# First mixer of an eight-layer kernel: reordering around the FIR filters, their sums on GpSimd, and bands with four channels innermost

## The chip, the cores and the metric

The kernel runs on one core of a Trainium2 chip, as one program. The metric is the device time of one execution in microseconds. The engines are PE (TensorE, its weight loads listed as PEld), DVE (VectorE), ACT (ScalarE), POOL (GpSimd) and SP (SyncE, which here only issues DMAs). Each engine works through its own queue in order; a DMA issued from SP's or ACT's queue runs on the core's 16 DMA engines.

## The reference

Four pairs of a token mixer and a feed-forward layer act on `x`, each as `x = x + layernorm(f(layernorm(x)))`. The change is in the first mixer only. `x` has 8 batches (the leading shape is 8 x 512 tokens x 256 channels here). Cut to what matters:

```python
q, k, v = (silu_short_conv(x @ W.T, conv) for each of the three)    # 4 taps, causal
delta = delta_rule_chunkwise(q, k, v, sigmoid(x @ Wb.T))            # 4 heads of 64; needs, per chunk of 32,
                                                                   # the inverse of a 32 x 32 triangle
fs, fm, fl = fir(v, 3 taps), fir(v, 15 taps), fir(v, 63 taps)       # causal, one filter per channel
g = softmax_with_floor(gate(x))                                    # 5 weights per head and token
o = g[0] * fs + g[1] * fm + g[2] * fl + g[3] * delta + g[4] * v
return rmsnorm(o) @ Wo.T
```

## The kernel before

The kernel is written in a tile framework. The order of the program text gives instructions their priority; a scheduler at compile time then orders each engine's queue, by what it takes to be ready, and places the semaphores. So an instruction can stand in its queue earlier than its text.

The mixer `l0_attn` has three stages, and `K.XA`, the buffer of the 8 batches of X (64 KB of each partition), is lent out in all of them.

**The front** (`front(b)`, 8 batches): normalisation and transposes, projections on PE, short convolutions on DVE (line 456), ACT's activations, shifted copies of v in `Vw` (line 488), and k k^T of every chunk in `S`, written to DRAM (`s_d`, lines 505 and 509). `front` is a generator and yields 11 times a batch. Per batch the rows of gates and strengths go to DRAM as `rows_d` (line 469).

Each half of the batches has one **inverse**: `inverse(0)` uses `K.XA[:, 0:4]`, `inverse(1)` `K.XA[:, 4:8]`. Its generator loads 2 MB of `s_d` (line 331) and the strengths `gb` from `g_d`, multiplies (line 343), makes 30 steps of a forward substitution on DVE (lines 351 and 354), multiplies again (line 357), and ends with a tail: an `affine_select` and a copy on POOL (lines 360 and 363), one 2 MB write to `t_d` on SP (line 364), and four times a transposing copy `tt` on ACT with a 512 KB write to `tt_d` on ACT's queue (lines 367 and 368; two buffers). `strengths(g)` makes `g_d` for a half: two loads from `rows_d`, a Tanh on ACT, four operations of DVE, four writes on SP (lines 377 to 388). `inverse(0)` starts after batch 3 and takes one step at each yield of batches 4 to 7, tail included. `strengths(1)` follows batch 7.

**The filters** (`filters(g)`, 32 groups of 8 channels). Channels are filtered as matmuls: lhsT is a strided slice of `Vw` (64 columns), rhs a band matrix of taps. The bands live in DRAM as `fd` and are read in windows by `load_toep` into three rotating tiles `toep` (two of them lie in `K.XA[:, 4:8]`). A tile has 4 filters (short, middle, long, identity) x 64 shifts x 8 channels, channels innermost, so one channel's 256 columns lie 8 floats apart:

```python
rhs=toep[g % NB_T][:, :, :, c],
```

Two matmuls of 64 columns each (r = 0, 1) go to the two halves of a PSUM bank. Per half group DVE multiplies the bank with the gates `gt` (line 632, tile `pr`, two buffers), then DVE adds the four products in two steps, `s1` (line 638) and `s2` (line 640), and ACT's queue writes `s2` to `f_d` (line 642). PSUM has 6 banks for this, so three groups. The gates of a head (`gates(h)`, lines 567 to 585) come from `rw_all`, which two DMAs load from `rows_d` (line 553). `scaled_v` (line 612) writes `v_d` every fourth group. After group 0 `load_tt` loads the transposed inverses of batches 0 and 1 (line 401).

After the last group the text has, in this order: `inverse(1)` started (its 2 MB read first), the four X loads of the first half, the buffers of the back half, and the loads of batches 0 and 1.

**The back half** (`back(b)`): the two halves of each inverse are joined (tile `W`, line 741, and `TT`, line 755), then the sequential part per batch; `inverse(1)` takes one step in two turns of the loop and is finished by force before batch 4's loads.

Of the kernel before, what the change touches and what calls it, by code (L numbers as in the profile page):

```python
# [9 lines left out]
F32 = mybir.dt.float32  # L10
# [264 lines left out]
def l0_attn(K):  # L275
# [6 lines left out]
    with ExitStack() as es:  # L282
# [45 lines left out]
        def inverse(g):  # L328
# [17 lines left out]
            for j in range(1, 31):  # L346
# [11 lines left out]
                both, both, blocks(gb, 0, (32, 2), (0, 32), (1, 32)), ALU.mult)  # L358
            yield
            nc.gpsimd.affine_select(  # L360
# [45 lines left out]
        with ExitStack() as e1:  # L406
            pv = pool(e1, "v", 1)
            Vw = pv.tile([P, NB, J, D], F32, name="Vw")
            with ExitStack() as ef:
# [11 lines left out]
                for f, (col, taps) in enumerate(((A_FS, 3), (A_FM, 15), (A_FL, 63))):  # L421
                    at = 1536 * f + 8 * (P - taps)
                    nc.sync.dma_start(
                        out=window(fd, 1536 * f, (4608, G), (1, 8 * (P - taps))),
                        in_=zero[:, 0:8 * (P - taps)])
                    nc.sync.dma_start(
                        out=window(fd, 1536 * f + 1024, (4608, G), (1, 512)), in_=zero[:, 0:512])
                    nc.sync.dma_start(
                        out=window(fd, at, (8, taps), (4608, G), (1, 8)),
                        in_=taps_T[col - A_FS:col - A_FS + taps].rearrange("u (g c) -> u g c", c=8))  # L430

# [80 lines left out]

                inv = iter(())
                for b in range(NB):
                    for _ in front(b):
                        next(inv, None)
                    if b % HALF == HALF - 1:
                        strengths(b // HALF, p1)
                    if b == HALF - 1:
                        inv = inverse(0)  # L520
                        next(inv)

            with ExitStack() as ef:
# [6 lines left out]
                for i in range(NB_T):  # L530
                    if i < 2:
                        t = K.XA[:, HALF + 2 * i:HALF + 2 * i + 2].rearrange(
                            "p b n d -> p (b n d)").rearrange("p (f t c) -> p f t c", f=4, c=8)
                    else:
                        t = p1.tile([P, 4, 64, 8], F32, name=f"toep{i}")
                    nc.gpsimd.memset(t, 0.0)
                    nc.vector.tensor_copy(
                        t[:, 3],
                        K.ident[:, 64:128, None][:, ::-1, :].to_broadcast([P, 64, 8]))
                    toep.append(t)  # L540

                def load_toep(g):
                    t = toep[g % NB_T]
                    nc.sync.dma_start(
                        out=t[:, 2].rearrange("p t c -> p (t c)"),
                        in_=window(fd, (3 * g + 2) * 1536, (8, P), (1, 512)))
                    nc.sync.dma_start(
                        out=t[48:128, 0:2].rearrange("p f t c -> p f (t c)"),
                        in_=window(fd, 3 * g * 1536 + 384, (8, 80), (1536, 2), (1, 512)))

# [67 lines left out]
                def filters(g):  # L618
# [3 lines left out]
                    for half in range(2):  # L622
                        ps = pmm.tile([P, 2, 4, 64], F32, tag="fir", name=f"pf{g}_{half}")
                        for m in range(2):
                            for r in range(2):
                                c = 4 * r + 2 * half + m
                                nc.tensor.matmul(
                                    ps[64 * r:64 * r + 64, m],
                                    lhsT=Vw[:, :, :, 8 * g + c].rearrange("p b j -> p (b j)"),
                                    rhs=toep[g % NB_T][:, :, :, c],  # L630
                                    start=True, stop=True)
                        nc.vector.tensor_tensor(
                            pr[:, 2 * half:2 * half + 2], ps[:, :, :, ::-1],
                            gt[:, h, None].to_broadcast([P, 2, 4, 64]), ALU.mult)
                    if g + NB_T < G:
                        load_toep(g + NB_T)
                    s1 = p1.tile([P, 4, 2, 64], F32, tag="s1", name=f"s1_{g}")
                    nc.vector.tensor_tensor(s1, pr[:, :, 0:2, :], pr[:, :, 2:4, :], ALU.add)
                    s2 = p2.tile([P, 4, 64], F32, tag="s2", name=f"s2_{g}")
                    nc.vector.tensor_tensor(s2, s1[:, :, 0, :], s1[:, :, 1, :], ALU.add)  # L640
                    for r in range(2):
# [4 lines left out]
                gates(0)  # L646
                given = False
                for g in range(G):
# [7 lines left out]
                    if g % 4 == 3:  # L656
                        scaled_v(g // 4)
                    if next(inv, 0) == 0 and not given:
                        given = True
                        for b in range(2):  # L660
                            load_tt(b)
        assert given
        inv = inverse(1)
        next(inv)
        K.load_x(K.i["x"], range(HALF))

# [206 lines left out]
        K.log_exp = True  # L873
        ahead = {b: loads(b) for b in range(2)}
        live, done, begun, steps = [back(0, *ahead[0])], 0, 1, 0
        while live:
# [1754 lines left out]
```

## Time and profile before

| | |
|---|---|
| median of 3 runs | 4565.85 us (4554.68 to 4568.97) |
| profiled execution | 4579.0 us, its span 4577.3 us |
| busy in the span | PE 3989.2 (87%), DVE 2710.9 (59%), POOL 2043.3 (45%), ACT 1982.9 (43%) |
| mean granted TensorE clock | 0.925 |
| the first mixer | from the start to about 710 us of the span |
| filters | first matmul at 248.8 us, last DVE product at 387.5 us |
| back half | first matmul at 402.7 us |

Times in the profile are microseconds from the span's start unless marked ns. A row of a group gives line, engine, operation, out<-in, shapes and count, then busy time and the mean ns of one, then the idle time of the engine before them and what ended it. In the timeline a row has its start, its length, the engine and in brackets the idle time before it and its releaser; SPq and ACTq are DMA issues. One fp32 matmul stands as two records.

### The profile page before, as it was taken

The page shows a single profiled execution, that of the slowest core. Times are in us where ns is not written, and L with a number is a line of the kernel's source. Part 1 is how long each engine was busy: PE and PEld are TensorE (multiplying, and loading weights), DVE is VectorE, ACT ScalarE, POOL GpSimd, SP SyncE. Part 2 cuts the span into 40 slices and gives each one's busy share as a digit, 9 for nine tenths or more (in the row PEclk, how much of TensorE's full clock was granted, in tenths as well). Part 3 has the DMA queues.
Part 4 walks back from the last instruction along what each step waited for, and adds up shares of the span by engine and source line. Part 5 has one row for each costly group of instructions (what it writes and reads, how often), then busy time and mean ns, then how long its engine had stood idle before and what let it go on. Part 6 is the DMA issues. An engine that isn't in the chain of part 4 may idle for free. (4 is left out here: it accounts for less than half of the span.)

```text
span 4577.3 us, 63200 instructions
## 1 busy us (share of the span) xinstructions
PE 3989.2 (87%) x21672; PEld 2642.3 (58%) x21672; DVE 2710.9 (59%) x7215; ACT 1982.9 (43%) x4082; POOL 2043.3 (45%) x2013
## 2 busy tenths in 40 slices
PE   8887898999998599789999978898988866899997
PEld 3435675555555399644454544565655544678884
DVE  7677656456647611255566534888888899721115
ACT  5511433444344233334444444767676655311112
POOL 0000322444344234345555423889888879223321
PEclk9897998999999799889999989999999986899999
DMA  4467621000000199500000002344333434236653
GB/s 117 142 180 193 174 50 45 18 10 6 7 5 20 52 249 251 148 5 10 6 6 6 1 23 67 122 125 127 124 123 121 125 106 138 93 121 230 228 182 113
DMA packets 389361, 442.89 MB, mean 97 GB/s; under 512 B 147469, under 2 KB 271487, under 8 KB 388527
## 3 DMA queue, kind: packets, MB, share of 16 engines
q1 hardware_dynamic: 361087, 390.18, 28.4%
q0 software_dynamic: 16272, 31.87, 2.6%
q10 hardware_dynamic: 11680, 16.80, 1.1%
q8 instruction: 172, 2.82, 0.3%
q14 instruction: 150, 1.23, 0.1%
HBM read 372.49 MB, written 66.26 MB: 96 GB/s over the span
## 5 line engine op out<-in xcount | busy, mean ns | idle before, releaser
L2046 POOL TENSOR_TENSOR h<-h,C 128x1024 f32<-128x1024 f32 x256 | 613.5, 2409 | 137.6 <-DVE h L2042 95.0
L2042 DVE TENSOR_TENSOR_SCAN h<-dA,dB 128x512 f32<-128x512 f32 x480 | 568.1, 1208 | 91.0 <-ACT dA L2030 77.3
L1000 POOL TENSOR_SCALAR p<-p,rs 128x128 f32<-128x128 f32 (+3 forms) x256 | 275.9, 1085 | 416.5 <-DVE rs L999 260.5
L2030 ACT ACTIVATE dA<-dl,A 128x512 f32<-128x512 f32 x480 | 330.5, 690 | 174.4 <-DVE h L2042 173.6
L1566 DVE CUSTOM_DVE_ANT_0 junk<-S,mask 128x256 f32<-128x256 f32 (+3 forms) x512 | 249.5, 487 | 195.1 <-PE S L1560 156.8
L2059 PE MATMUL y<-C,h 128*128 128x128 f32 x2048 | 295.3, 295 | 73.0 <-POOL h L2046 72.8
L2059 PEld LDWEIGHTS y<-C,h 128*128 128x128 f32 x2048 | 260.2, 153 | 158.5 <-POOL h L2046 102.9
L1594 ACT ACTIVATE PT<-T 128x128 f32<-128x128 f32 (+3 forms) x512 | 198.1, 435 | 278.9 <-PE T L1589 267.9
L1560 PE MATMUL S<-KZ,QT 64*128 64x512 f32 (+3 forms) x1024 | 260.1, 491 | 23.8 <-DVE mx L1566 23.6
L2258 PE MATMUL gb<-xbT,w_b 128*128 128x256 f32 (+1 forms) x1472 | 255.3, 332 | 1.0 <-ACT ts L2462 0.6
L2258 PEld LDWEIGHTS gb<-xbT,w_b 128*128 128x128 f32 x1472 | 230.2, 191 | 23.1 <-ACT ts L2462 0.8
L2264 DVE TENSOR_TENSOR hTb<-sb,gb 128x512 f32<-128x512 f32 x71 | 48.8, 687 | 325.4 <-PE gb L2258 314.1
L2025 POOL TENSOR_TENSOR dB<-du,B 128x1024 f32<-128x1024 f32 x96 | 233.8, 2436 | 0.1
L1844 PE MATMUL pf<-fT,w_l_ffn 128*128 128x512 f32 x384 | 206.6, 676 | 28.5 <-ACT fT L1838 11.3
L1589 PE MATMUL T<-QT,KZ 64*128 64x384 f32 (+3 forms) x1024 | 217.1, 465 | 2.9 <-ACT PT L1594 2.5
L2025 DVE TENSOR_TENSOR dB<-du,pb 128x1024 f32<-128x1024 f32 x160 | 191.2, 1195 | 23.4 <-ACT pb L2023 21.3
L182 POOL TENSOR_TENSOR X<-X,yn 128x256 f32<-128x256 f32 (+1 forms) x56 | 79.7, 1441 | 263.0 <-ACT yn L177 233.1
L1334 ACT ACTIVATE hT<-h,w_l_ffn 128x128 f32<-128x128 f32 x384 | 109.5, 368 | 198.0 <-PE h L1329 198.0
L1329 PE MATMUL h<-xgT,w 128*128 128x128 f32 x1536 | 185.1, 279 | 0.0
L1560 PEld LDWEIGHTS S<-KZ,QT 64*128 64x128 f32 x1024 | 116.7, 193 | 114.0 <-issue 58.3
L1597 POOL TENSOR_SCALAR_AFFINE_SELECT PT<-PT 128x512 f32<-128x512 f32 x128 | 81.3, 635 | 219.1 <-ACT PT L1594 206.2
L998 ACT ACTIVATE p<-p,nm 128x128 f32<-128x128 f32 (+3 forms) x256 | 143.5, 561 | 80.7 <-DVE nm L994 72.7
(587 smaller groups left out, 9147.0 us busy)
## 6 DMA issues: line engine op xcount, KB each, us to landing
w_b<-l3f_w SPq DMA_DIRECT2D x138, 512.0 KB
C<-xdd SPq DMA_DIRECT2D x256, 256.0 KB
B<-xdd SPq DMA_DIRECT2D x256, 256.0 KB
w<-l1f_w SPq DMA_DIRECT2D x48, 1024.0 KB
w<-l1f_w SPq DMA_DIRECT2D x48, 256.0 KB
X<-x SPq DMA_DIRECT2D x16, 512.0 KB
c<-ys SPq DMA_DIRECT2D x16, 512.0 KB
X<-l0fd SPq DMA_DIRECT2D x22, 320.0 KB
```

Source lines behind the costliest of these rows:

```text
L1000: nc.gpsimd.tensor_scalar(p[:, 0:n], p[:, 0:n], rs, None, ALU.mult)
L1560: nc.tensor.matmul(ps[:, 0:n], lhsT=QT[half, qt * P:n], rhs=KZ[half, j % 2, 0:n], start=True, stop=True)
L1566: nc.vector.tensor_tensor_reduce(out=junk[:, 0:n], in0=ps[:, 0:n], in1=mask[:, L - n:L], scale=1.0, scalar=-3.0e38, op0=ALU.add, op1=ALU.m ...
L1589: nc.tensor.matmul(ps[:, 0:n], lhsT=KZ[half, j % 2, kt * P:(kt + 1) * P], rhs=QT[half, kt * P:L], start=True, stop=True)
L1594: nc.scalar.activation(PT[:, j, :], ps[:, 0:n], AF.Exp)
L1844: nc.tensor.matmul(ps, lhsT=gu[:, k, j * 768 + c * P:j * 768 + (c + 1) * P], rhs=R[b]["fT"][:, k, :], start=(k == 0), stop=(k == 1))
L2025: on.tensor_tensor(dBs[k], R[b]["du", h], B[:, None, :].to_broadcast([P, 2, L]), ALU.mult)
L2030: nc.scalar.activation(dA, R[b]["dl", h][:, c, :], AF.Exp, scale=A[:, 2 * h + c, n:n + 1])
L2042: nc.vector.tensor_tensor_scan(hs[k][:, c, :], dA, dBs[k][:, c, :], 0.0, ALU.mult, ALU.add)
L2046: nc.gpsimd.tensor_tensor(hs[k], hs[k], row_C.pop(k)[:, None, :].to_broadcast([P, 2, L]), ALU.mult)
L2059: nc.tensor.matmul(R[b]["y", h][q // 2][:, q % 2, c * P:(c + 1) * P], lhsT=t[:, c, q * P:(q + 1) * P], rhs=K.ident, is_transpose=True, sta ...
L2258: nc.tensor.matmul(ps[:, q, :], lhsT=ww[:, k, (c + q) * P:(c + q + 1) * P], rhs=xT[:, k, :], start=(k == 0), stop=(k == 1))
```

## The change

Five things are changed in `l0_attn`. (1) `inverse` yields True ahead of its tail; the front stops stepping `inverse(0)` there, and the rest, with `load_tt` for batches 0 and 1, is run after group 1 of the filters. (2) `strengths(1)` is called after group 21 in place of after batch 7. (3) The X loads of the first half and the start of `inverse(1)` stand behind the loads of batches 0 and 1. (4) `s1` and `s2` are added on GpSimd. (5) The bands have their 8 channels split into two blocks (one for each r) of 64 shifts x 4 channels, so that a channel's columns lie 4 floats apart; `fd` is written with 16-byte pieces and read with 1 KB pieces.

```diff
@@ inverse
             nc.vector.tensor_tensor(
                 both, both, blocks(gb, 0, (32, 2), (0, 32), (1, 32)), ALU.mult)
-            yield
+            yield True
             nc.gpsimd.affine_select(
...
@@ the writes of fd
-                    at = 1536 * f + 8 * (P - taps)
+                    n = 4 * (P - taps)
                     nc.sync.dma_start(
-                        out=window(fd, 1536 * f, (4608, G), (1, 8 * (P - taps))),
-                        in_=zero[:, 0:8 * (P - taps)])
+                        out=window(fd, 1536 * f, (4608, G), (768, 2), (1, n)),
+                        in_=zero[:, 0:2 * n].rearrange("g (q n) -> g q n", q=2))
                     nc.sync.dma_start(
-                        out=window(fd, 1536 * f + 1024, (4608, G), (1, 512)), in_=zero[:, 0:512])
-                    nc.sync.dma_start(
-                        out=window(fd, at, (8, taps), (4608, G), (1, 8)),
-                        in_=taps_T[col - A_FS:col - A_FS + taps].rearrange("u (g c) -> u g c", c=8))
+                        out=window(fd, 1536 * f + 512, (4608, G), (768, 2), (1, 256)),
+                        in_=zero[:, 0:512].rearrange("g (q n) -> g q n", q=2))
+                    for q in range(2):
+                        nc.sync.dma_start(
+                            out=window(fd, 1536 * f + 768 * q + n, (4, taps), (4608, G), (1, 4)),
+                            in_=taps_T[col - A_FS:col - A_FS + taps].rearrange(
+                                "u (g q c) -> u g q c", q=2, c=4)[:, :, q])
...
@@ the loop over the front
                 inv = iter(())
+                inverted = True
                 for b in range(NB):
                     for _ in front(b):
-                        next(inv, None)
-                    if b % HALF == HALF - 1:
-                        strengths(b // HALF, p1)
+                        inverted = inverted or next(inv)
                     if b == HALF - 1:
+                        strengths(0, p1)
                         inv = inverse(0)
-                        next(inv)
+                        inverted = next(inv)
+                assert inverted
...
@@ bands
-                        t = p1.tile([P, 4, 64, 8], F32, name=f"toep{i}")
+                        t = p1.tile([P, 4, 2, 64, 4], F32, name=f"toep{i}")
...
                     nc.sync.dma_start(
-                        out=t[:, 2].rearrange("p t c -> p (t c)"),
-                        in_=window(fd, (3 * g + 2) * 1536, (8, P), (1, 512)))
+                        out=t[:, 2].rearrange("p q t c -> p q (t c)"),
+                        in_=window(fd, (3 * g + 2) * 1536, (4, P), (768, 2), (1, 256)))
                     nc.sync.dma_start(
-                        out=t[48:128, 0:2].rearrange("p f t c -> p f (t c)"),
-                        in_=window(fd, 3 * g * 1536 + 384, (8, 80), (1536, 2), (1, 512)))
+                        out=t[48:128, 0:2].rearrange("p f q t c -> p (f q) (t c)"),
+                        in_=window(fd, 3 * g * 1536 + 192, (4, 80), (768, 4), (1, 256)))
...
@@ filters
-                                    rhs=toep[g % NB_T][:, :, :, c],
+                                    rhs=toep[g % NB_T][:, :, r, :, 2 * half + m],
...
-                    nc.vector.tensor_tensor(s1, pr[:, :, 0:2, :], pr[:, :, 2:4, :], ALU.add)
+                    nc.gpsimd.tensor_tensor(s1, pr[:, :, 0:2, :], pr[:, :, 2:4, :], ALU.add)
...
-                    nc.vector.tensor_tensor(s2, s1[:, :, 0, :], s1[:, :, 1, :], ALU.add)
+                    nc.gpsimd.tensor_tensor(s2, s1[:, :, 0, :], s1[:, :, 1, :], ALU.add)
...
@@ the loop over the groups
-                    if next(inv, 0) == 0 and not given:
-                        given = True
+                    if g == 1:
+                        for _ in inv:
+                            pass
                         for b in range(2):
                             load_tt(b)
-        assert given
-        inv = inverse(1)
-        next(inv)
-        K.load_x(K.i["x"], range(HALF))
+                    if g == 21:
+                        strengths(1, p1)
...
@@ ahead of the back half
         ahead = {b: loads(b) for b in range(2)}
+        K.load_x(K.i["x"], range(HALF))
+        inv = inverse(1)
+        next(inv)
```

More of the change, by code (lines that the diff above doesn't have):

```diff
@@ L532, in l0_attn @@
                         t = K.XA[:, HALF + 2 * i:HALF + 2 * i + 2].rearrange(
-                            "p b n d -> p (b n d)").rearrange("p (f t c) -> p f t c", f=4, c=8)
+                            "p b n d -> p (b n d)").rearrange(
+                                "p (f q t c) -> p f q t c", f=4, q=2, c=4)
                     else:
-                        t = p1.tile([P, 4, 64, 8], F32, name=f"toep{i}")
+                        t = p1.tile([P, 4, 2, 64, 4], F32, name=f"toep{i}")
                     nc.gpsimd.memset(t, 0.0)
@@ L538, in l0_attn @@
                         t[:, 3],
-                        K.ident[:, 64:128, None][:, ::-1, :].to_broadcast([P, 64, 8]))
+                        K.ident[:, None, 64:128, None][:, :, ::-1, :].to_broadcast([P, 2, 64, 4]))
                     toep.append(t)
@@ L646, in l0_attn @@
                 gates(0)
-                given = False
                 for g in range(G):
```

## The prediction

> **What bounds the kernel now.** The change touches only the first mixer, so I read stretches of it, then the waits inside. The first two rows below are two batches of the front (batch 1, and batch 7); the others are the start of the filters, their steady part, and the gap before the back half. Columns: stretch and length, busy us of PE, PEld, DVE, ACT, POOL (with counts), PE clock, DMA share, GB/s.
>
> ```profile
> 38.56:64.83 26.27, 24.55 (x96) 11.73 (x96) 18.57 (x46) 16.16 (x28) 0.21 (x1) 0.94 0.30 74
> 202.38:241.60 39.22, 29.83 (x96) 14.65 (x96) 15.26 (x23) 23.38 (x32) 3.85 (x3) 0.78 0.62 196
> 256.00:279.00 23.00, 5.04 (x22) 2.08 (x20) 18.89 (x41) 2.11 (x3) 1.80 (x1) 0.66 0.93 263
> 279.00:388.00 109.00, 107.92 (x464) 46.74 (x460) 83.88 (x164) 0.94 (x2) 0.00 (x0) 0.98 0.64 193
> 388.00:403.00 15.00, 0.30 (x12) 0.34 (x14) 8.46 (x18) 1.28 (x1) 4.27 (x11) 0.55 0.81 238
> ```
>
> PE sets the front (24.6 of 26.3 us) and the filters (107.9 of 109). Three places break that: batch 7, 13 us longer than batch 1; the start of the filters; and the 15 us before the back half.
>
> Batch 7 first, by ACT's timeline:
>
> ```profile
> 206.12 3.77 ACT L367 COPY tt<-X 128x1024 f32<-128x1024 f32 x2 [0.60 <-POOL X L363]
> 213.73 1.91 ACT L367 COPY tt<-X 128x1024 f32<-128x1024 f32 x1 [2.81 <-DMA l0tt<-tt]
> 216.04 1.95 ACT L367 COPY tt<-X 128x1024 f32<-128x1024 f32 x1
> ```
>
> The four transposing copies that end `inverse(0)` sit in ACT's queue between the copies that empty PE's banks, and the third waits for a write of the first to land; DVE then waits 22.7 us in one piece for ACT (L454).
>
> PE's timeline at the start of the filters, and SP's:
>
> ```profile
> 248.84 7.71 PE L627 MATMUL pf<-X,Vw 128*64 128x256 f32 x32 [1.05 <-ACT S L502]
> 266.37 3.98 PE L627 MATMUL pf<-toep,Vw 128*64 128x256 f32 x16 [9.81 <-DVE rw_all L567]
> 278.50 7.68 PE L627 MATMUL pf<-X,Vw 128*64 128x256 f32 x32 [8.15 <-DVE pr L632]
> 251.81 3.95 SPq L388 DMA_DIRECT2D l0g<-bts  x4
> 257.21 1.16 SPq L553 DMA_DIRECT2D rw_all<-l0rows  x2
> ```
>
> PE fills its banks, then idles 9.8 + 8.2 = 18 us for the gates, whose input `rw_all` is issued only behind the four writes of `strengths(1)`.
>
> In the steady part, groups by line (busy, mean ns | idle before):
>
> ```profile
> L627 PE MATMUL pf<-X,Vw 128*64 128x256 f32 x320 | 76.4, 645 | 8.6 <-DVE pr L632 8.6
> L632 DVE TENSOR_TENSOR pr<-pf,gt 128x512 f32<-128x512 f32 x63 | 42.8, 685 | 16.5 <-PE pf L627 16.5
> L638 DVE TENSOR_TENSOR s<-pr 128x512 f32<-128x512 f32 x31 | 21.1, 681 | 0.0
> L640 DVE TENSOR_TENSOR s<-s 128x256 f32<-128x256 f32 x30 | 12.4, 412 | 4.1 <-DMA l0f<-s 4.1
> ```
>
> PE never waits for DVE for long there, and DVE's pr waits for PE. The pace is in the timeline of PE's weight loads:
>
> ```profile
> 301.35 0.20 PEld L627 LDWEIGHTS pf<-X,Vw 128*64 128x64 f32 x2 [0.26 <-issue]
> 301.82 0.20 PEld L627 LDWEIGHTS pf<-X,Vw 128*64 128x64 f32 x2 [0.26 <-issue]
> ```
>
> A pair of half-width matmul records starts every 0.465 us. A group has 8 matmuls of two records each, so 8 pairs: 8 x 0.465 = 3.72 us. Elsewhere pairs and fours of column halves run side by side at the speed of one: L1611's records of 256 contiguous columns come in fours 0.22 us apart, L193's singly 0.216. So these bands, read 32 bytes apart, cost 2.15 times a contiguous read.
>
> **The change part by part.** The profiled execution took 4579.0 us (span 4577.3, 1.7 around it), 13 above the median 4565.85 of the runs; I work out differences in the former and take them off the latter. A measurement can tell about 0.3%, 13.7 us, from nothing.
>
> *Tail of `inverse(0)`, moved behind group 1.* It issues POOL 4.07 + 0.37 us, a 2 MB write on SP, four ACT copies (7.7 us) and four 512 KB writes on ACT's queue; behind it `load_tt` puts four loads on SP. Batch 7 loses its excess over batches 1 to 3 (26.3, 25.3, 26.5; mean 26.0): 39.2 - 26.0 = 13.2 us at most. But text order is only a priority here: three loads of X, written behind the filters, were issued at 218 us, so the copies may be pulled forward into gaps of ACT in batch 7. I take 10, bounds 0 and 13.2. In the filters the tail stands ahead of the f_d issues on ACT's queue and of POOL's sums: 7.7 + 4.4 us once, against a cover of three groups in PSUM (3 x 3.72 = 11 us) and an ACT busy 0.94 of 109 us. Charge 0; without the cover 4.
>
> *`strengths(1)`, moved to group 21.* It takes two loads and four writes (3.95 us of issue) off SP and 2.7 us of DVE from ahead of `rw_all`. The last S write ends its issue at 251.6 and `rw_all` starts at 257.2: gain 5.6 at most; 4 taken, since the buffers of the old pool must still be drained; low end 0. At group 21, SP has 0.75 us of issue per 3.72 us and ACT is idle, so the six DMAs, a Tanh (0.41) and up to two table loads (1.28 each, as at 268.8) hide; if they stand ahead of a band load they cost up to 4.
>
> *`load_x` and the 2 MB read of `inverse(1)` behind the loads of batches 0 and 1.* SP's waits:
>
> ```profile
> SPq L702 <- DMA l0v<-vs: 8.4, 1, 8.4
> ```
>
> The TS load waits 8.4 us for the 512 KB write of v, which shares the engines with that 2 MB read (issued 387.45; v 389.74); PE then starts 15.3 us late. With the read behind, v's write lands earlier: gain 0 to 8.4. The X loads were early anyway. I take 6.
>
> *Sums on POOL.* Removed from DVE: 0.68 + 0.41 per group. On POOL, nearest rows:
>
> ```profile
> L1459 POOL TENSOR_TENSOR X<-X,yl 128x512 f32<-128x512 f32 x16 | 19.9, 1267 | 2.3 <-ACT yl L1456 2.3
> L182 POOL TENSOR_TENSOR X<-X,yn 128x256 f32<-128x256 f32 x32 | 22.1, 724 | 18.6 <-ACT yn L177 18.6
> ```
>
> 1.27 + 0.72 = 2.0 us per group, under PE's 3.72, so hidden; DVE was hidden too, so nothing is won. After the last group the sums end 2.0 - 1.1 = 0.9 us later, ahead of an F that is not the first thing needed: 0, at worst 0.9.
>
> *Four channels innermost.* Bands now step 16 bytes. No row has this. Ends: 0.465 us per pair (as at 32 bytes) and 0.216 (contiguous). Other strided rows: Vw's weights, 1 KB apart, load 64 columns in 197 ns against 136 in L846; the tt copy, 256 bytes apart, takes 1.93 us for 1024 elements where two contiguous 128x512 copies (L148) take 1.23. The slowdown is about the same from 32 bytes to 1 KB, so it does not grow with the step, and 16 is nearer to 32 than to 4. I take 0.465: gain 0. [...]
>
> The band loads go from 288 packets of 2 KB to 576 of 1 KB: by the trace 84 ns and 46 ns a packet, so 1.51 to 1.66 us of the 16 engines per group, at a share of 0.64: hidden at 3.72 us. The set-up has 12 writes in place of 9, and 16-byte pieces, at 15 to 24 us, long before the first band load at 143: 0.
>
> Sum: -10 - 4 - 6 = **-20 us, 4546**.
>
> **The rivals.**
>
> *Bands free at 16 bytes.* PE then needs 8 x 0.216 = 1.72 us per group, and next are DVE 2 x 0.685 + 0.26 = 1.63, POOL 2.0, DMA 0.64 x 3.72 + 0.15 = 2.53, at the 0.93 reached at 256 to 279 about 2.7. Gain 29 groups x (3.72 - 2.7) = 30 (at POOL's 2.0, 50). With the 20: -50, **4516**. For it: contiguous rows run at 0.216. Against: every strided row is slow. 0.33.
>
> *Nothing takes hold.* The scheduler pulls the tail forward and issues the 2 MB read first as before, since only it is ready when PE ends: within 6 us, **4562**. 0.08.
>
> *Slower: the first step of `inverse(1)` blocks DVE.* Its 2.29 us product (L343) waits for the 2 MB read, now behind the loads of batches 0 and 1, some 6.3 MB: at 253 GB/s 25 us. DVE executes in order, and behind the product queue the W and TT copies (L741, L755) of batch 0, for which PE waits. The read would land near 374 (end of PE's filters) + 2 + 25 + 8 = 409, where W was copied at 405 before: the 20 are gone and 4 lost, and a tail of `inverse(1)` so much later holds up batch 4 by some 10: +14, **4580**. It decides if the product is queued ahead of L741. Against: steps come one in two turns of the back. 0.17.
>
> **How the numbers follow.** My case 0.42 (own range 4534 to 4563: of its gains the front may be 0, or all at their upper ends), rivals 0.33, 0.08, 0.17. Faster by over 13.7 us: 0.33 and 0.30 of my case, 0.63. Within: 0.11 of mine, 0.06 of the second, 0.17. Slower: 0.17 and 0.03 of tails, 0.20. The range runs from 4506 (bands free, DMA better than 2.7) to 4580, leaving out some 0.15.
>
> **What would show it.** Batch 7 at 27 to 30 us; `rw_all` issued within 3 us of the last S write; L627 pairs still 0.465 us apart; POOL sums 2.0 us per group and PE never waiting for them; TS issued within 6 us of the last pf. Pairs at 0.22 to 0.3 show the first rival; a DVE wait of 10 us or more for X<-l0s ahead of L741 the last. My sum is wrong if the tt copies still stand inside batch 7, or if PE waits for band loads.

## The result: slower by 20 us, and the profile after

The changed kernel takes 4586.35 us in the median of 7 runs (4580.82 to 4594.27) against 4566.48 (7 runs): ratio 1.0049, 95% interval 1.0037 to 1.0060. Its profiled execution took 4583.64 us, span 4581.9; that of before, at 4579.0, was longer than all seven of its timed runs, so the two traces differ by less than the medians, and places are compared by what lies between them. Lines of the changed kernel count 3 to 5 more than before (627 is now 632, 740 is 743).

Both ends of the filters first. Stretches of the changed kernel: batch 7, the filters from 260 us on (the second of the two stalls at their start lies in it), and the gap before the back half (columns as in the prediction).

```profile
201.08:232.57 31.49, 25.21 (x96) 12.30 (x96) 14.99 (x23) 22.80 (x32) 3.86 (x3) 0.89 0.73 234
260.00:381.70 121.70, 107.35 (x466) 49.27 (x464) 77.96 (x123) 2.64 (x4) 68.00 (x62) 0.94 0.70 204
381.70:396.70 15.00, 3.49 (x138) 3.25 (x140) 1.39 (x2) 0.58 (x1) 6.67 (x14) 0.57 0.78 210
```

Batch 7 lasts 31.5 us in place of 39.2. ACT's timeline shows that the four copies were pulled forward into it, but further apart than before:

```profile
204.83 1.94 ACT L367 COPY tt<-X 128x1024 f32<-128x1024 f32 x1 [0.61 <-POOL X L363]
213.46 3.86 ACT L367 COPY tt<-X 128x1024 f32<-128x1024 f32 x2
220.54 2.00 ACT L367 COPY tt<-X 128x1024 f32<-128x1024 f32 x1 [1.08 <-DMA l0tt<-tt]
```

PE's and SP's timelines at the start of the filters:

```profile
239.81 7.57 PE L632 MATMUL pf<-X,Vw 128*64 128x256 f32 x32 [1.05 <-ACT S L505]
256.16 3.91 PE L632 MATMUL pf<-toep,Vw 128*64 128x256 f32 x16 [8.79 <-DVE rw_all L575]
268.17 7.18 PE L632 MATMUL pf<-X,Vw 128*64 128x256 f32 x30 [8.10 <-DVE pr L637]
...
241.14 1.37 SPq L512 DMA_DIRECT2D l0s<-S  x1
246.43 1.14 SPq L558 DMA_DIRECT2D rw_all<-l0rows  x2
```

The first matmul comes 9.0 us earlier. The stalls are 16.9 us in place of 18.0: `rw_all` is issued 3.9 us behind the S writes where it was 5.6.

The filters from 260 us on, groups by line (the 8.1 us of PE are the second stall), and PE's weight loads:

```profile
L643 POOL TENSOR_TENSOR s<-pr 128x512 f32<-128x512 f32 x31 | 43.7, 1409 | 61.0 <-DVE pr L637 32.0 <-DMA X<-x 20.4 <-DMA gb<-l0g 8.1
L637 DVE TENSOR_TENSOR pr<-pf,gt 128x512 f32<-128x512 f32 x63 | 42.7, 686 | 41.6 <-PE pf L632 39.4 <-POOL s L643 2.0
L632 PE MATMUL pf<-toep,Vw 128*64 128x256 f32 x146 | 35.6, 640 | 6.2 <-DMA toep<-l0fd 6.2
...
301.49 0.20 PEld L632 LDWEIGHTS pf<-X,Vw 128*64 128x64 f32 x2 [0.28 <-issue]
301.94 0.20 PEld L632 LDWEIGHTS pf<-X,Vw 128*64 128x64 f32 x2 [0.26 <-issue]
```

A pair still starts every 0.46 us. The sums take 1.41 + 0.79 us by the mean. New is one stall of PE of 6.2 us at 353 us, for a band load. Still, the filters end 5.7 us earlier (381.7 against 387.4).

Then the back half, SP's timeline, and DVE's first and last product of `inverse(1)`, first before, then changed:

```profile
387.45 0.34 SPq L331 DMA_DIRECT2D X<-l0s  x1
...
396.92 2.29 DVE L343 TENSOR_TENSOR X<-X,gn 128x2048 f32<-128x2048 f32 x1 [6.17 <-DMA X<-l0s]
473.55 2.28 DVE L357 TENSOR_TENSOR X<-X,gb 128x2048 f32<-128x2048 f32 x1
```
```profile
387.73 0.57 SPq L705 DMA_DIRECT2D TS<-l0t  x1
402.46 1.94 SPq L723 DMA_DIRECT2D bf<-l0f  x2
404.44 6.49 SPq L331 DMA_DIRECT2D X<-l0s  x1
...
438.10 2.27 DVE L343 TENSOR_TENSOR X<-X,gn 128x2048 f32<-128x2048 f32 x1
507.78 2.29 DVE L357 TENSOR_TENSOR X<-X,gb 128x2048 f32<-128x2048 f32 x1
```

TS is issued 6.0 us behind the last pf (the filters' last matmul), and PE's first pW (the matmul that opens a batch of the back half) comes at 392.1, 10.6 us earlier than before; 5.7 of these are the filters' earlier end. But the 2 MB read is issued 22.7 us behind the last pf, where before it came at once (387.45), and `inverse(1)` runs on DVE from 438 to 510 in place of 397 to 476. By their first pW the batches then begin at 392, 414, 448, 498, 551, 589, 621, 653 us; before at 403, 429, 469, 509, 541, 573, 606, 638. The lead of 21 us at batch 2 is 11 at batch 3 and a loss of 11 at batch 4; the mixer's last matmul (L193, 698.8 to 712.8) is 14.0 us late. Some 10 us of this lead are a low granted clock in batch 1 of the profile of before (last section). A profile with the same order of queues and without that low clock (the move alone, below) has its batches at 403, 428, 459, 499, 530, 563, 595, 627: against it the lead of 11 us at batch 2 is gone at batch 3, and the loss is 21 at batch 4 and 25 at the last, batch 7.

### The profile page after: what moved, and what is told of

Read it like the earlier page. It is cut to its first block, busy times and chain, and to the rows that moved or that the text cites. A ratio compares the mean times of both kernels' runs of the same rounds, so it can differ in the third digit from the quotient of the medians.

```text
span 4581.9 us, 63266 instructions
## 1 busy us (share of the span) xinstructions
PE 3991.2 (87%) x21672; PEld 2651.5 (58%) x21672; DVE 2693.8 (59%) x7151; ACT 1981.6 (43%) x4082; POOL 2115.9 (46%) x2077
## 5 line engine op out<-in xcount | busy, mean ns | idle before, releaser
L2264 PEld LDWEIGHTS gb<-xbT,w_b 128*128 128x128 f32 x1472 | 230.2, 191 | 23.1 <-ACT ts L2468 0.8
L2501 POOL DMA_INDIRECT ys<-yb,place x71 | 70.1, 987 | 239.1 <-ACT yb L2500 224.9
```

What stands on the lines that cost most here:

```text
L2264: nc.tensor.matmul(ps[:, q, :], lhsT=ww[:, k, (c + q) * P:(c + q + 1) * P], rhs=xT[:, k, :], start=(k == 0), stop=(k == 1))
```

## The experiments

All ratios are to runs of the kernel before on the same chip; 0.001 is 4.6 us. After the first four the question was which part makes the loss, then what the rest is worth, then how the loss comes about.

### Which part

**`inverse(1)` put back ahead of the loads**, the rest of the change kept:

```diff
+        inv = inverse(1)
+        next(inv)
+        K.load_x(K.i["x"], range(HALF))
         p1, p2 = pool(es, "ba", 1), pool(es, "bb", 2)
...
-        K.load_x(K.i["x"], range(HALF))
-        inv = inverse(1)
-        next(inv)
```

> The changed kernel with one part undone: the start of inverse(1) (its 2 MB read, gb, gn) and load_x stand again right behind the filters, ahead of the loads of batches 0 and 1. My theory, read from the two traces: the late start of inverse(1) costs the time. Its first product went from 396.9 to 438.1 us and its last from 473.6 to 507.8, so POOL's affine_select came at 510 in place of 478, the transposed copies at 518 to 531 in place of 485 to 494, and batch 4, whose TT and T1 are read from those writes, began 53 us behind batch 3 in place of 32. With the start put back the first product should come at 385 to 400, batch 4 should follow batch 3 within 35 us, and the time should be the 4566 of before less the 5.7 us by which the filters now end earlier: 4561, within 5. Rival: the loss lies in something else that the trace shows only late (the sums on POOL, the other layout of the bands, code); then the time stays at 4580 to 4590, and the step from batch 3 to batch 4 shrinks without the end moving.

Measured 1.0001 (0.9991 to 1.0011), 4564.68 us. The first product came at 394.3, batch 4 followed batch 3 by 31.6 us. So the late `inverse(1)` is worth some 22 us (1.0049 against 1.0001).

**Before, with that move alone** (the same three lines moved the other way):

> The kernel before with one part of the change alone: load_x and the start of inverse(1) behind the loads of batches 0 and 1. My theory: this part alone makes it slower. The back half begins earlier by up to 10 us (in the changed kernel its first matmul came 10.6 us earlier, of which the filters' earlier end was 5.7, so 5 is this part's), but the first product of inverse(1) comes 35 to 45 us later, and batch 4 then 15 to 25 us later than before: 4582 to 4590. Rival (the reasoning of my prediction): the gain of 5 at the start of the back half stays and batch 4 has slack; then 4560 to 4566.

Measured 0.9998 (0.9987 to 1.0009): my theory failed here. SP's timeline says why:

```profile
387.10 0.34 SPq L331 DMA_DIRECT2D X<-l0s  x1
389.29 0.30 SPq L696 DMA_DIRECT2D T<-l0t  x1
```

The read is still the first: moved in the text, it was not moved in the queue. Something else in the change had to let the text position take hold.

**The changed kernel with the sums back on DVE** (`nc.gpsimd` to `nc.vector` in `s1` and `s2`):

> The changed kernel with the two sums of each group back on DVE; inverse(1) still stands behind the loads in the text. The run of the kernel before with the move alone showed that the text position by itself moves nothing: the 2 MB read was still issued at 387 us, first of its neighbours. My new theory: the order written for SP is made from when each transfer is thought to be ready, and text order decides only between those that are ready; with the sums on GpSimd the loads of batch 0 are thought to be ready as early as the read, and then the text decides. So with the sums on DVE the read should again be issued ahead of the loads (within 2 us of the last pf), its first product come within 15 us, batch 4 follow batch 3 within 35 us, and the time fall to 4560 to 4568. Rival: another part (strengths(1) at group 21, the tail behind group 1, the bands) makes the read late; then it is still issued some 20 us behind the last pf and the time is 4580 to 4590.

Measured 0.9985 (0.9975 to 0.9995). The read was issued at 377.92, as the last pf ended:

```profile
377.92 0.34 SPq L331 DMA_DIRECT2D X<-l0s  x1
380.11 0.30 SPq L702 DMA_DIRECT2D T<-l0t  x1
389.06 0.65 SPq L705 DMA_DIRECT2D TS<-l0t  x1
```

**Before, with the move and the sums on GpSimd, nothing else**:

> The kernel before with two parts of the change and no other: the move of inverse(1) behind the loads, and the sums on GpSimd. By the theory of the interaction these two alone make the loss: read issued some 20 us behind the last pf, first product at 435 to 445, affine_select of inverse(1) held at 505 to 520, batch 4 20 us later than before, and 4583 to 4595 in all (the changed kernel's 4586 plus the 0 to 6 us by which its filters end earlier). Rival: the sums are free and the read early, or the late read has slack in the order of before: 4562 to 4568.

Measured 1.0066 (1.0052 to 1.0079), the slowest of all:

```profile
406.54 1.27 SPq L699 DMA_DIRECT2D TS<-l0t  x1
407.86 1.26 SPq L702 DMA_DIRECT2D TS<-l0s  x1
415.25 5.78 SPq L331 DMA_DIRECT2D X<-l0s  x1
```

The read again stands 23.5 us behind the last pf (391.7). So two parts make the loss together: the move alone does nothing, with the sums on DVE it does nothing either, and the sums without the move (1.0001 with `inverse(1)` put back, against 0.9985 with the sums on DVE) are worth some 7 us. That the scheduler's estimate of readiness is what the sums alter is an inference from these orders; the order itself is shown.

### The ends of the filters and the stall

**The tail of `inverse(0)` alone** (before, with `yield True` and the rest run after group 1):

> The kernel before with one part alone: the tail of inverse(0) behind group 1, strengths(1) where it was. My prediction gave it 10 us. In the changed kernel the first matmul of the filters came 9.0 us earlier than before, but with inverse(1) put back only 5.1 and with the contiguous bands 3.6 earlier. Theory: 3 to 9 us at the filters' first matmul, kept to the end: 4557 to 4563. Rival: the tail now delays the filters' own work (load_tt and the copies stand ahead of the f_d issues), or batch 4's start is set by inverse(1), not by the filters: 4564 to 4568.

Measured 1.0000 (0.9990 to 1.0009): nothing. PE's timeline shows where it went:

```profile
246.71 7.71 PE L629 MATMUL pf<-X,Vw 128*64 128x256 f32 x32 [0.96 <-ACT S L502]
269.46 3.98 PE L629 MATMUL pf<-toep,Vw 128*64 128x256 f32 x16 [15.05 <-DMA gb<-l0g]
...
260.57 1.14 SPq L555 DMA_DIRECT2D rw_all<-l0rows  x2
262.57 0.34 SPq L546 DMA_DIRECT2D toep<-l0fd  x1
...
279.81 1.88 DVE L634 TENSOR_TENSOR pr<-pf,gt 128x512 f32<-128x512 f32 x3
```

The filters' first matmul came 2.1 us earlier, but the first stall grew from 9.8 to 15.05 us: with `strengths(1)` still ahead of it, `rw_all` was issued 11.2 us behind the S writes, before 5.7. The releaser named, the read of `gb`, feeds nothing that PE needs here. The 16 records that end this stall are group 2's, and start 10 us before DVE's first product, so they wait for no bank; they read the third band tile, whose load SP issued behind `rw_all` (in the version to beat both, below, the trace names that load for this stall, 13.59 us). It is the second stall that waits for the gates, and it ends with DVE's first product, at 280.5 in place of 278.4.

**Both moves at the ends**, tail and `strengths(1)`, nothing else:

> The kernel before with the two moves at the ends of the filters, the tail of inverse(0) behind group 1 and strengths(1) at group 21, and no other part; inverse(1) ahead of the loads, sums on DVE, bands of eight. With the tail alone PE stood 15.0 us for rw_all at the start of the filters, where before and the run with the sums back on DVE had 9.8 and 8.6. Theory: the two moves need each other: strengths(1) away frees SP for rw_all, so the first matmul comes at 240 to 242, the two stalls are 8.6 and 8.0, the filters end at 378 to 381 and the time is 0.9985 to 0.9992 of before. Rival: the gain of the run with the sums on DVE (0.9985) came from the bands of four; then this run stays at 0.9996 to 1.0005.

Measured 0.9982 (0.9971 to 0.9992), -8 us. Stalls of 9.31 and 8.01 us, filters' end 381.4. The two moves need each other, and they make the gain of the run with the sums on DVE (0.9985): the bands of four added nothing to it that shows.

**The eight `l0pq` writes on ACT's queue**, on the version with `inverse(1)` put back (`nc.sync` to `nc.scalar` in `query_scales`):

> The changed kernel with inverse(1) put back ahead of the loads, and the eight writes l0pq issued by ACT. With the sums on GpSimd every run but those with wider reads showed one stall of PE of 5.7 to 6.2 us late in the filters (353, 357, 363 us), with SP in the issue of l0pq (6.0 to 8.6 us) and the band loads behind it; with the sums on DVE it was 1.2. Theory: this stall is the price of the sums on GpSimd in the filters, through the order on SP; without it the filters take 136 to 137 us in place of 142 and the time is 5 us below the 1.0001 of before that inverse(1) put back gave: 0.9985 to 0.9993. Rival: the f_d writes on ACT now wait behind l0pq, GpSimd waits for its buffers and PE for DVE: as many us, 1.000.

Measured 0.9971 (0.9960 to 0.9982). The filters took 136.7 us in place of 142.0. SP's timeline in the changed kernel had shown what stood in the way:

```profile
348.71 6.01 SPq L604 DMA_DIRECT2D l0pq<-rqy  x8
354.81 0.38 SPq L549 DMA_DIRECT2D toep<-l0fd  x1
```

With the sums on DVE the same eight writes took 3.62 us, at 364.8, and PE had no stall of 1 us behind them. The trace gives 5 us for this edit; the medians give some 14, of which 9 are not explained.

### The bands

**Contiguous reads of the band tile** (64 neighbours in place of 64 numbers 16 bytes apart):

```diff
-rhs=toep[g % NB_T][:, :, r, :, 2 * half + m],
+rhs=toep[g % NB_T][:, :, r].rearrange("p f t c -> p f (t c)")[
+    :, :, 64 * (2 * half + m):64 * (2 * half + m) + 64],
```

> The changed kernel with each band operand of L637 read as 64 contiguous numbers in place of 64 numbers 16 bytes apart, from the same tile, after the same loads; the numbers are other ones, so the filters' values are not the reference's, and only the time is of use. It prices the step of 16 bytes by itself. My theory: the pair of half-width records goes from 0.458 to about 0.216 us, as in the contiguous rows elsewhere, and the group is then bound by POOL's sums (2.04 us) or by the band loads (2.5 to 2.7 us); the filters take 32 x 1.0 to 1.6 us less, 30 to 50 us. Rival: the pair's pace has another cause than the step (PE's two halves, the 64 columns of weights 1 KB apart, 0.197 us per load); then the pair stays over 0.4 us and the filters end at the same time as in the changed kernel.

Measured 1.0019 (1.0009 to 1.0030). Weight loads, eight pairs in one row:

```profile
304.92 1.63 PEld L632 LDWEIGHTS pf<-X,Vw 128*64 128x64 f32 x16 [0.71 <-issue]
```

1.63 / 8 = 0.204 us a pair: the step is the cause. But the filters took 128.6 us, only 13.3 less: PE stood some 50 us in place of 23.1, and 27.2 us of it, from 280 to 370 us, for band loads (groups by line: 11.5 + 15.7).

**Two channels innermost** (`q=4, c=2` in the writes of `fd`, the tiles and the loads):

> The changed kernel with two channels innermost in place of four: bands step 8 bytes, and the band loads go in pieces of 512 bytes, 1152 packets a group. [...] If the slowdown goes with the bytes passed over, as a stream of bytes would, the pair halves from the 0.458 of a 16-byte step, or the 32-byte step would have been slower than the 16-byte one, which it was not (0.465 and 0.458). Rival: any step that isn't 4 bytes costs the same; then the pair stays at 0.46, and the smaller packets (1152 by 30 to 40 ns over 16 engines, 2.2 to 2.9 us a group under 3.66) hide: the time of the changed kernel, within 5 us.

Measured 1.0055 (1.0040 to 1.0070):

```profile
305.38 1.72 PEld L632 LDWEIGHTS pf<-toep,Vw 128*64 128x64 f32 x16 [2.76 <-DVE wgm L584]
...
54.43 0.63 PE L479 MATMUL prt<-C,rw 32*128 32x32 f32 x4 [16.34 <-ACT rw L471]
```

A pair takes 0.215 us at 8 bytes (1.72 / 8), nearly as when contiguous: the rival's 0.46 fell. By the step, the pair took 0.465 us at 32 bytes (before), 0.458 at 16 (the changed kernel), 0.215 at 8 and 0.204 at 4 (the contiguous reads). Nearly all of the cost goes between 16 and 8 bytes; what makes it, no run shows. The filters took 134.9 us, but the four last tap writes, in 8-byte pieces, kept SP 16.9 us, and batch 0's `rw`, which shares the taps' buffer, waited 16.3.

**A version to beat both**: the two-channel bands, taps in their own buffer, set-up behind batch 0 in the text, `strengths(1)` at group 17, `inverse(1)` first:

> A version meant to beat both: inverse(1) ahead of the loads, two channels innermost (a record takes 0.39 us at 8 bytes against 0.64 at 16), the taps in a buffer of their own so that batch 0 doesn't wait for their writes (16.3 us of PE in the first run of that layout), the set-up behind batch 0 in the text, and strengths(1) at group 17. Theory: the front starts as in the changed kernel, the filters take 130 to 135 us in place of 142, now bound by the band loads (share of the transfers over 0.9), and the end comes 7 to 12 us earlier than the 4564.7 of the run with inverse(1) put back: 4553 to 4558. Rival: the 8-byte writes of the taps (10368 pieces) still fill the transfer engines while batch 0's q and rows wait behind them on SP: part of the 16 us stays, 4560 to 4575.

Measured 0.9978 (0.9969 to 0.9988). **The same with `l0pq` on ACT's queue**:

> The version with two channels innermost, with one more edit: the eight writes l0pq are issued by ACT in place of SP. In that version PE stood 8.4 us at 349 us, where SP issued those eight writes with three groups' band loads behind them. Theory: the stall goes, the filters take 126 to 129 us in place of 134.8, and the time is 4548 to 4552 where the version without the edit had 0.9978 of before, so 0.9962 to 0.997. Rival: the band loads are bound by the transfer engines (share over 0.9), so that what the issue loses is made up by nothing: the stall is spread over later groups and the time stays within 2 us of 0.9978.

Measured 0.9959 (0.9943 to 0.9975), 4549.64 us: the fastest of all, against both kernels. The filters took 130.1 us, short of the 126 to 129 expected; of PE's waits the first is

```profile
PE pf L635 <- DMA X<-l0fd: 18.3, 9, 4.6
```

### How the lateness costs

**bq on DVE** in the changed kernel:

> The changed kernel with the product bq of each batch on DVE in place of GpSimd. In the changed kernel bq of batch 3 (514.2 us) and with it the l0pq reads of batch 4 on SP (490 to 517) stood behind the affine_select of inverse(1) on GpSimd, which waited for DVE's last product (507.8). Two ways in which the late inverse(1) can cost: through TT and T1 of batch 4, which are written behind affine_select (my theory: then this edit lets batch 3 go on earlier but batch 4 begins at 545 to 553 as before, 1.003 to 1.005), or through GpSimd's queue, which holds bq of batch 3 (rival: then batch 4 begins at 530 to 540 and the time falls to 0.999 to 1.002).

Measured 1.0021 (1.0011 to 1.0031). Batch 4 began at 547, as I held, and the time fell to about what the rival held: neither was the whole.

**`load_x` and `inverse(1)` between the loads of batches 0 and 1**:

> The changed kernel with load_x and the start of inverse(1) between the loads of batch 0 and those of batch 1. The dose of lateness is halved: the read is issued some 8 us behind the last pf in place of 23, and its first product should come at 410 to 420 in place of 438. Theory: batch 0 keeps its early start (392) and the tail of inverse(1) is early enough for batch 4: 0.998 to 1.001, no worse than the version with inverse(1) first. Rival: any read behind the loads of batch 0 loses the place among DVE's and GpSimd's work, and the time is 1.003 to 1.005 as in the changed kernel.

Measured 1.0035 (1.0022 to 1.0047): my theory failed. The first product came at 418.9, 25 us later than with `inverse(1)` first in place of 44, and that cost 16 us in place of 22: most of the loss is there with half the lateness.

**No batch needs `inverse(1)`** (changed kernel; the rows of `tt_d` and `t_d` read are those of `b % HALF`), **and the control** with `inverse(1)` first:

> The changed kernel with other data: batches 4 to 7 read TT, T1 and TS of inverse(0) (rows of batch b - 4) in place of inverse(1), so no batch waits for inverse(1), which still runs in full; the values of batches 4 to 7 are not the reference's. If the wait of batch 4 for the writes of inverse(1) is the loss (my theory), batch 4 follows batch 3 within 38 us in place of 53 and the time falls to 0.998 to 1.001 of before. If the loss is the work of inverse(1) itself, which shares DVE and GpSimd with batches 1 to 3 at another place (49.8 us from batch 2 to 3 at a granted clock of 0.66 in the changed kernel), batch 4 begins no more than 8 us earlier and the time is 1.003 to 1.006.

> The same other data in the version with inverse(1) put back ahead of the loads: a control. There the last product of inverse(1) came at 455 us and batch 4 began 31.6 us behind batch 3, so nothing should wait: within 4 us of the 1.0001 that that version had, 0.999 to 1.001. If it falls by more than 6 us, batch 4 waited there too, and what the run above gains is not all the lateness.

Measured 1.0046 (1.0032 to 1.0060) and 1.0002 (0.9993 to 1.0011). Batch 4 still followed batch 3 by 48.4 us. My theory that the loss is batch 4's wait for TT and T1 fell, with one doubt: SP's queue still held batch 4's other loads.

**Neither need nor queue**, and **the queues alone**, with the true data:

```diff
-            nc.gpsimd.tensor_tensor(qT, qT, PQ, ALU.mult)
+            nc.vector.tensor_tensor(qT, qT, PQ, ALU.mult)
...
-            nc.sync.dma_start(out=t_d[g * P:(g + 1) * P, :], in_=flat)
+            (nc.gpsimd if g else nc.sync).dma_start(out=t_d[g * P:(g + 1) * P, :], in_=flat)
...
-                    K.load_x(K.i["x"], range(HALF, NB))
+                if begun == HALF + 2:
+                    K.load_x(K.i["x"], range(HALF, NB))
```

> The run with other data (batches 4 to 7 read the rows of batches 0 to 3, so their values are not the reference's) left 1.0046, and its trace shows why: nothing of batch 4 needed inverse(1) any more, but SP stood from 485 to 514 us in front of the l0t write, and again at 530 in front of load_x of the upper half, with batch 4's TS, k, q, PQ, V and F behind them, and GpSimd held bq behind affine_select. So here nothing is queued behind inverse(1) either: the l0t write of inverse(1) is issued by GpSimd, load_x of the upper half comes two batches later, and bq is made on DVE. Theory (waits, through data or through a queue, are the loss): batch 4 begins 31 to 38 us behind batch 3 and the time is 0.997 to 1.001, though the read is as late as in the changed kernel. Rival (the work of inverse(1) beside batches 1 to 3 and the lower clock are the loss): 1.002 to 1.005, with the granted clock from 450 to 570 us still at 0.6 to 0.8.

> The same edits of the queues with the true data: batch 4 needs TT and T1 of inverse(1) again. The run with bq alone on DVE had 1.0021. Theory: the data wait stays (batch 4 begins at 540 to 550), what stands behind it on SP is smaller, 1.000 to 1.003: the difference to the run above is the price of the wait for TT and T1 itself, 2 to 10 us. Rival: SP's queue was the whole loss, and this run is within 2 us of the one above.

Measured 1.0050 (1.0034 to 1.0065) and 1.0032 (1.0022 to 1.0041). With nothing waiting, batch 4 still came 44.9 us behind batch 3, and the time shows no gain. The trace does show one. From the last pf to the mixer's last matmul the changed kernel took 331.1 us, without the need for the data 328.9, with neither need nor queue 321.9, and with bq alone on DVE 315.0; with `inverse(1)` first it was 294.8 and, in the control, 298.0 (307 to 311 in four profiles that have the read first and a low clock in batch 1). The layers behind the mixer are the same code in all; they took 3869.1 us in the profile of the changed kernel and 3879.5 with neither need nor queue, which hides the 9 us won. So the need for the data is worth little, the queues 9 to 16 us, and a part of the loss is left.

What else the lateness moves is the work. DVE in the changed kernel and with `inverse(1)` first, in the first 30 us of the back half, then from batch 2 to batch 3 (third busy column, after PE and PEld):

```profile
390.00:420.00 30.00, 23.59 (x363) 20.78 (x364) 5.94 (x13) 5.73 (x11) 4.69 (x2) 0.65 1.04 276
448.20:498.00 49.80, 44.18 (x379) 34.89 (x378) 40.53 (x74) 11.85 (x24) 11.16 (x6) 0.66 0.26 70
```
```profile
390.00:420.00 30.00, 15.47 (x266) 13.56 (x266) 23.32 (x40) 4.88 (x9) 4.49 (x7) 0.63 0.92 241
450.60:490.90 40.30, 32.63 (x395) 25.00 (x394) 24.06 (x68) 19.87 (x30) 15.47 (x8) 0.92 0.54 177
```

The DVE rows of lines 343 to 357 add up to some 40 us in either. With the read first they fill a DVE that has nothing else to do while the loads come in; with the read late DVE is idle 24 of 30 us there, and the work then lies beside three batches (40.5 busy of 49.8).

**The 30 steps left out**, on the kernel with neither need nor queue:

```diff
-            for j in range(1, 31):
+            for j in range(1, 1 if g else 31):
```

> The run with nothing waiting for inverse(1) (1.0050), with the 30 steps of inverse(1) left out (its values are other ones; the read, the first and the last product, affine_select, the copies and writes stay). Those steps are 60 instructions and about 36 of its 38 to 41 us on DVE. With inverse(1) ahead of the loads they ran from 394 to 457 us, where PE waits for loads anyway; in the changed kernel DVE stood nearly idle from 390 to 438 (0.4 to 5 us busy of 10) and ran them from 438 to 510 beside batches 1 to 3. My theory now: this work on DVE beside the batches is what remains of the loss. Then batch 2 to 3 takes 40 us or less in place of 48 to 50, batch 3 to 4 some 32, and the time falls to 0.993 to 0.998. Rival: the granted clock falls by itself after the read (0.5 at 450 to 480), whatever DVE does: 1.002 to 1.005 again with the clock at 0.5 to 0.7 there.

Measured 1.0001 (0.9992 to 1.0010): 22 us less than the same kernel with the steps, the size of the whole loss (from the last pf to the mixer's last matmul 304.3 us in place of 321.9). The time expected was missed. Batches 2 to 3 and 3 to 4, with the steps, then without:

```profile
447.20:495.20 48.00, 41.73 (x384) 32.54 (x382) 42.53 (x91) 12.34 (x26) 5.91 (x4) 0.72 0.37 88
495.20:540.10 44.90, 33.84 (x383) 25.96 (x382) 28.53 (x90) 19.89 (x30) 11.60 (x7) 0.85 0.58 165
```
```profile
453.10:499.40 46.30, 40.72 (x386) 31.60 (x386) 21.93 (x64) 15.97 (x28) 5.83 (x4) 0.71 0.70 183
499.40:531.60 32.20, 29.25 (x384) 23.55 (x382) 20.23 (x62) 12.43 (x26) 5.84 (x4) 1.00 0.54 125
```

Batch 3 to 4 came down from 44.9 to 32.2 us, but batch 2 to 3 only from 48.0 to 46.3, though DVE's work there fell from 42.5 to 21.9 us: PE was busy for 40.7 us of it at a granted clock of 0.71. Batch 1 to 2 even took 40.1 us in place of 33.2. So a low clock stands between batches 2 and 3 with the steps or without, and what the steps cost shows behind it. A kernel with the read first and without the steps was not run, so that they are free in their old place is read from the idle DVE there, not shown.

## Why the prediction was wrong, point by point

- **Bands: right.** Taken 0.465 us a pair, measured 0.458. The first rival had the wrong step, and the wrong size: with free reads the filters won 13 us, not 30, since PE stood 27.2 us for band loads that the 2.7 us a group of the sum took as hidden.
- **Tail of `inverse(0)`: the place was right (9.0 us at the first matmul for 10; 3.5 to 9.0 in the profiles with the same front), the sum was not.** Alone it is worth nothing, since the stalls at the filters' start take it back; **with `strengths(1)`** the two are worth 8 us (3.7 to 13.2) where I added 10 and 4. Batch 7 took 31.5 us for 27 to 30, and `rw_all` came 3.9 us behind the S writes, for 3. The 18 us of PE were read as one wait for the gates; the first 9.8 are a wait for the third band tile, though the gates, which come last, do set when PE goes on.
- **Sums on GpSimd at 0: wrong twice.** The sums (2.2 us a group for 2.0) are hidden as said, but the order on SP changed with it: the `l0pq` writes in front of the band loads cost 5.7 to 6.6 us of PE in every profile with the sums there, bands of four or eight, and these writes on SP. And it let the next part take hold.
- **`load_x` and the read of `inverse(1)` at -6: the step that failed.** I priced what goes ahead (TS came at 6.0 us, as said, and pW 10.6 us earlier, of which 4.9 are this part's) and not what falls behind: the first product of `inverse(1)` went from 397 to 438 us, and with it 40 us of DVE work, of which 26 had lain ahead of 440 us and 2 lie there now. Its price was 22 us, 28 from my term. With it the sum would have been -8 + 5 + 22 = +19; measured +20 (17 to 27 by the interval). The 22 are taken from the changed kernel itself; two other runs, move and sums without the rest (+30) and the two moves at the ends (-8), add up to +22. How the lateness costs is shown in part only: the 30 steps are worth 22 us where they lie late, and the queues behind `inverse(1)` 9 to 16 us of the mixer, so the two overlap or part of it is clock.
- **The rival on the slow side** had the right edit and the wrong reason. The first product stood behind L744 of batch 0 (394.69), so it blocked nothing there; and the late tail that "holds up batch 4" could be taken away, data and queue, without a gain in time (1.0050), though bq alone off GpSimd's queue gave 13 us (1.0021). I also let it be decided by that one place in DVE's order, and gave it 0.17.
- **"Nothing takes hold"** was true of this part by itself (0.9998), and untrue with the sums moved.
- **The range.** The low end of my case, 4534, does not follow from its terms: their upper ends (13.2, 5.6 and 8.4) add up to 27.2 us, 4539.
- Both signs that the prediction named for a wrong sum appeared: the copies stand inside batch 7, and PE waits for band loads. They account for the smaller errors, not for the large one.

What stays open: why bq on DVE alone (1.0021) does better than the kernel that has it and two waits fewer (1.0050; the traces put 7 us of it in the mixer's back half and 11 behind the mixer), and how much of batches 2 to 4 is DVE's time and how much the granted clock.

## What to carry to other kernels

When a long chain of work on one engine is moved behind something, ask which idle time it filled and what will lie beside it in its new place; here the transfers that it let pass gained 4.9 us at the first pW, and the move cost 22 in all. Where text order is only a priority, price parts in pairs: a part that does nothing alone can decide what another one does, and here the move alone showed no effect at all, and the pair cost 30 us. An engine's load moved to an idle engine is not free if it changes the order of a third queue (here the `l0pq` writes, at 5.7 to 6.6 us of PE): look at what DMA issues will stand ahead of the steady loads.

## What the runs showed of the hardware

**The granted clock made two kinds of batch 1.** Between the starts of batches 1 and 2, with the same 357 to 359 matmul records, stretches of two versions:

```profile
416.50:456.10 39.60, 37.56 (x357) 29.71 (x356) 24.98 (x52) 9.69 (x19) 3.65 (x3) 0.66 0.53 110
```
```profile
421.60:450.60 29.00, 25.81 (x357) 20.20 (x356) 26.72 (x53) 9.69 (x19) 5.20 (x4) 1.00 0.82 172
```

The first is `inverse(1)` put back with `l0pq` on ACT, the second without that edit. Four profiles with the read first (before among them) took 39.6 to 40.4 us at 0.64 to 0.66, six took 29.0 to 30.6 at 0.94 to 1.00; that is about the spread of one kernel's runs (4556.8 to 4574.58 us for the second). In the profile of before the longest gap of PE in the 15 us ahead of that stretch is 2.93 us (before L818, for DVE's R); no run here tells what set the low clock off.

**Tap writes in small pieces held up the queue that issued them.** The four tap writes of the longest filter in 8-byte pieces kept SP 16.9 us where 16-byte pieces (two writes, half as many pieces) took 3.5:

```profile
27.36 16.90 SPq L430 DMA_DIRECT2D l0fd<-taps_T  x4
```
```profile
25.48 3.49 SPq L430 DMA_DIRECT2D l0fd<-taps_T  x2
```
